# Moving a sum to VectorE, staggering the last weight preparations and re-weighting the list schedule of a four-layer graph kernel

## The chip, the cores and the metric

One core of a Trainium2 chip runs the whole program. The metric is the device time of that core in microseconds (us), from the first to the last instruction of one execution. Engines are named as in the profile: PE is TensorE (PEld its weight loads), DVE is VectorE, ACT is ScalarE, POOL is GpSimd, SP is SyncE, which issues all DMA transfers here.

## The reference

Four graph layers are applied one after the other to 128 graphs of 64 nodes with 512 features, each followed by a residual and a normalisation over the features. All is fp32.

```python
x = _layernorm(x + _L0_gnn_ref(x, adj, w, a))                    # A @ x @ w, A from tanh/exp of x@w@a
x = _layernorm(x + _L1_gnn_ref(x, adj, Wq, bq, Wk, bk, Wv, bv))  # adj*exp(q k^T), normalised, @ v
x = _layernorm(x + _L2_gnn_ref(x, adj, nodemask, Wqk, Wv))       # a softmax weight per node, times x @ Wv
x = _layernorm(x + _L3_gnn_ref(x, adj, W1, b1, gamma, beta, W2, b2))
# _L3: relu(hypergraph_conv(x, adj, W1, b1)) (512 -> 1024), layer_norm,
#      hypergraph_conv(h, adj, W2, b2) (1024 -> 512), + x
```

## The kernel before

Two tiles of 128 rows (four graphs) make a group; there are 32 groups, and the adjacency is prepared for two groups at a time (a "chunk"). Each large product (left side times weights) is made in Strassen's way: the left side and the weights are cut into 2 x 2 blocks, four sums are formed of the left blocks and four of the weight blocks, and seven products replace eight. Sums of the weights are made once, stored in DRAM, and then streamed through a ring of buffers for every group. Products with `v2` (layer 2), `3a` and `3b` (layer 3) take stored weights; those of `m1` and `m2` stay on the chip.

The program is a list of operations with a cost and a key, which a list scheduler written in the kernel orders when it is built. It decides, per engine, the fixed order of the instructions, and which buffer each value gets. The costs only set that order: on the chip each engine takes its instructions in the order found, and waits in front of each until its inputs and its buffer are there.

```python
class Order:
    LATENCY = {"PE": 260, "DVE": 110, "ACT": 130, "POOL": 160, "SP": 2200}   # ns until others see a result
    BYTES_PER_NS = 230
    AHEAD = 3.5
    ...
def w_dve(n):  return 165 + n * 33 // 32      # ns of an operation on n elements per partition
def w_act(n):  return 175 + n * 27 // 32
def w_pool(n): return 200 + n * 9 // 4
    ...
    kind("x", 6, GT, D)
    kind("k4", 13, PIECE)       # 13 buffers of 128 x 1024 fp32: raw weights, transposed x, sums, z, v
    kind("ring", 8, PIECE)      # streamed weights
    ...
def side_sums(a, s, n):                       # the four sums of the left side
    def do(engine, out, left, right, add=False):
        def emit():
            e = nc.vector if engine is dve else nc.gpsimd
            (e.tensor_add if add else e.tensor_sub)(out[1](), left[1](), right[1]())
        engine(n, [left[0], right[0]], [out[0]], emit)
    do(dve, s[0], a["21"], a["22"], True)
    do(pool, s[2], a["11"], a["21"])
    do(dve, s[1], s[0], a["11"])
    do(dve, s[3], a["12"], s[1])

def stored_in_place(which, b, n, width):      # b: the raw quarters, which lie in k4 buffers
    store = in_dram(which, width)
    for k in USE:
        if k[0] == "b": store(k, b[k])        # a DMA to DRAM
    t = {"t1": b["b11"], "t3": b["b12"], "t2": b["b22"], "t4": b["b21"]}
    combine(b, t, n)                          # the sums, in place: three on DVE, one on POOL
    for k in USE:
        if k[0] == "t": store(k, t[k])
    ...
order.key = 7.0
stored_in_place("v2", quarter_views(raw(wv2, 2), D), D, HALF)   # two k4 buffers
order.key = 8.0
stored_in_place("3a", quarters(w3a), PIECE, PIECE)              # four k4 buffers
order.key = 9.0
w3b_q = quarters(w3b)                                           # four more
...                                     # PE: a row of beta times w3b (7 us); DVE: gamma times w3b, in place
stored_in_place("3b", w3b_q, PIECE, PIECE)
    ...
def normalized(...):                          # bn_stats, bn_aggr on DVE, a power on POOL, then ACT:
    act(n // n_stats + 60, ...)               # x * rstd + nm
```

A group goes through steps 0 to 15 of its own (0 to 2 layer 0, 3 to 6 layer 1, 7 to 11 layer 2, 12 to 15 layer 3), and a new group starts every four steps, so about four groups are under way at once. The steps that the prediction speaks of: 7 transposes the normalised x, 8 multiplies by `m2`, 11 by `v2`, 12 gathers the normalised x over the graph (PE, output `bank<-g_bd,x`), 13 multiplies by `3a`, 14 gathers the normalised h (`bank<-g_bd,h`), 15 multiplies by `3b`.

Of the kernel before, what the change touches and what calls it, by code (L numbers as in the profile page):

```python
# [12 lines left out]
AF = mybir.ActivationFunctionType  # L13
# [3 lines left out]
P = 128  # L17
B, N, D, DH = 128, 64, 512, 1024
# [8 lines left out]
PIECE = 1024  # L27
# [25 lines left out]


class Order:
    LATENCY = {"PE": 260, "DVE": 110, "ACT": 130, "POOL": 160, "SP": 2200}
    BYTES_PER_NS = 230
    AHEAD = 3.5

# [107 lines left out]


def w_dve(n):
    return 165 + n * 33 // 32  # L170


def w_act(n):
# [8 lines left out]
def kernel(  # L182
# [23 lines left out]
    nc = tc.nc  # L206
# [10 lines left out]
    def kind(name, n, *shape, space=None):  # L217
        kinds[name] = [(space or sbuf).tile([P, *shape], FP, name=f"{name}{i}") for i in range(n)]

    kind("x", 6, GT, D)  # L220
    kind("k4", 13, PIECE)
    kind("ring", 8, PIECE)
    kind("h", 1, GT, DH)
    kind("k2", 3, D)
# [11 lines left out]
    order = Order({k: len(v) for k, v in kinds.items()})  # L236

    def const(t_, cells=1):
        b = Buf(None, cells)
        b.t = t_  # L240
        return b
# [5 lines left out]
    def dve(n, reads, writes, emit, urgent=0.0):  # L247
        order.add("DVE", w_dve(n), reads, writes, emit, urgent)

    def act(n, reads, writes, emit, urgent=0.0):  # L250
        order.add("ACT", w_act(n), reads, writes, emit, urgent)
# [52 lines left out]
    def load_adj(c):  # L304
        order.key = APART * GC * c - 7.0 if c else -10.5
        adjs[c] = Buf("adj")
        load(adjs[c], adjT[:, ts(c, CT * N)], lambda t_: t_.rearrange("p t i -> p (t i)"))


    def raw(w, n, kind_="k4"):  # L310

        made = []
        v = w.rearrange("(h c p) o -> h p c o", h=n, p=P)
        for h in range(n):
            b = Buf(kind_, 2)
            order.add("SP", 60, [], [b], lambda b=b, h=h: nc.sync.dma_start(out=rows_of(b, w.shape[1]), in_=v[h]),
                      size=4 * P * 1024)
            made.append(b)
        return made

    def rows_of(b, cols):
        return b.t.rearrange("p (c o) -> p c o", o=cols)
# [51 lines left out]
    HALF = PIECE // 2  # L374
# [11 lines left out]
    def quarter_views(bufs, cols):  # L386

        return {
            f"b{h + 1}{i + 1}": (
                bufs[h][i],  # L390
                lambda h=h, i=i: rows_of(bufs[h], cols)[:, :, ts(i, cols // 2)],
            )
            for h in range(2) for i in range(2)
        }
# [3 lines left out]
    def in_dram(which, width):  # L398
        n = PIECE // width
        tiles = []  # L400
        for i in range(-(-len(USE) // n)):
            tiles.append(const(dram.tile([P, PIECE], FP, name=f"{which}_{i}"), n))
        stored[which] = [(t_, min(n, len(USE) - n * i)) for i, t_ in enumerate(tiles)]

        def store(k, piece):
            i = USE.index(k)
            dst = tiles[i // n]

            def emit():
                src = piece[1]()  # L410
                d_ = dst.t[:, ts(i % n, width)].rearrange("p (c o) -> p c o", c=src.shape[1])
                nc.sync.dma_start(out=d_, in_=src)

            order.add("SP", 60, piece[0] if isinstance(piece[0], list) else [piece[0]], [dst[i % n]], emit,
                      size=P * width * 4)

        return store

    def stored_in_place(which, b, n, width):

        store = in_dram(which, width)
        for k in USE:
            if k[0] == "b":
                store(k, b[k])
        t = {"t1": b["b11"], "t3": b["b12"], "t2": b["b22"], "t4": b["b21"]}
        combine(b, t, n)
        for k in USE:
            if k[0] == "t":
                store(k, t[k])
# [64 lines left out]
    m2 = gram("m2", wq2_raw, wk2_raw)  # L494

    order.key = 7.0
    stored_in_place("v2", quarter_views(raw(wv2, 2), D), D, HALF)

    def quarters(w):

        rows, cols = w.shape
        v = w.rearrange("(h c p) (i o) -> h i p c o", h=2, p=P, i=2)
        made = {}
        for h in range(2):
            for i in range(2):
                q = Buf("k4")
                order.add("SP", 60, [], [q],
                          lambda q=q, h=h, i=i: nc.sync.dma_start(out=rows_of(q, cols // 2), in_=v[h, i]),
                          size=P * PIECE * 4)
                made[f"b{h + 1}{i + 1}"] = (q, lambda q=q: rows_of(q, cols // 2))  # L510
        return made
# [7 lines left out]
    bw_b = const(sb("bw_b", D))  # L519
# [149 lines left out]
    def side_sums(a, s, n):  # L669


        def do(engine, out, left, right, add=False):
            def emit():
                e = nc.vector if engine is dve else nc.gpsimd
                (e.tensor_add if add else e.tensor_sub)(out[1](), left[1](), right[1]())

            engine(n, [left[0], right[0]], [out[0]], emit)

        do(dve, s[0], a["21"], a["22"], True)
        do(pool, s[2], a["11"], a["21"])  # L680
        do(dve, s[1], s[0], a["11"])
        do(dve, s[3], a["12"], s[1])

    def left_side(xT):
        a = left_blocks(xT)
# [74 lines left out]
    def normalized(reads_of, view, n_stats, eps, n):  # L760

        mv = Buf("col", GT)
        for t in range(GT):
            st = Buf("col", n_stats)
            for i in range(n_stats):
                dve(n // n_stats, [reads_of(t, i)], [st[i]], lambda t=t, i=i, st=st: nc.vector.bn_stats(
                    st.t[:, 6 * i : 6 * i + 6], view()[:, t, ts(i, n // n_stats)]))
            dve(12, [st], [mv[t]], lambda t=t, st=st: nc.vector.bn_aggr(mv.t[:, 2 * t : 2 * t + 2], st.t[:, : 6 * n_stats]))
        ve, rstd, nm = Buf("col"), Buf("col"), Buf("col")

        def pairs_of(b, i):
            return b.t[:, : 2 * GT].rearrange("p (t s) -> p t s", s=2)[:, :, i]

        dve(GT, [mv], [ve], lambda: nc.vector.tensor_scalar(ve.t[:, :GT], pairs_of(mv, 1), eps, None, ALU.add))
        order.add("POOL", 790, [ve], [rstd],
                  lambda: nc.gpsimd.tensor_tensor(rstd.t[:, :GT], ve.t[:, :GT], mhalf, ALU.pow))
        dve(GT, [mv, rstd], [nm], lambda: nc.vector.scalar_tensor_tensor(
            nm.t[:, :GT], pairs_of(mv, 0), -1.0, rstd.t[:, :GT], ALU.mult, ALU.mult))
        for t in range(GT):
            for i in range(n_stats):  # L780
                act(n // n_stats + 60, [reads_of(t, i), nm, rstd], [reads_of(t, i)], lambda t=t, i=i: nc.scalar.activation(
                    view()[:, t, ts(i, n // n_stats)], view()[:, t, ts(i, n // n_stats)], AF.Identity,
                    bias=nm.t[:, t : t + 1], scale=rstd.t[:, t : t + 1]))

# [25 lines left out]
    def z_into(zT, bias=None):  # L810


        def at(k):
            return xT_view(zT)[:, ts(int(k[1]) - 1, KC // 2), ts(int(k[0]) - 1, P)]

        def cell(k):
            return zT[GT * (int(k[1]) - 1) + int(k[0]) - 1]

        def two(ps):
            return ps().rearrange("p (c q) -> p c q", c=2)  # L820

        def first(k, token, ps):
            if bias is None:
                act(2 * P, [token], [cell(k)], lambda: nc.scalar.copy(at(k), two(ps)), NOW)
            else:
                for c in range(2):
                    col = 2 * (int(k[1]) - 1) + c
                    act(P, [token, bias], [cell(k)], lambda c=c, col=col: nc.scalar.activation(
                        at(k)[:, c], two(ps)[:, c], AF.Identity, bias=bias.t[:, col : col + 1]), NOW)

        def more(k, token, ps):
            dve(2 * P, [token, cell(k)], [cell(k)], lambda: nc.vector.tensor_add(at(k), two(ps), at(k)), NOW)

        return first, more


    def run(g):
        V, A = nc.vector, nc.scalar
# [121 lines left out]
        dve(GT, [mx], [mx], lambda: V.tensor_scalar(mx.t[:, :GT], mx.t[:, :GT], -SCALE, None, ALU.mult), NOW)  # L960
        e2 = Buf("e", GT)
        for t in range(GT):
            act(P, [ps_p, mx], [e2[t]], lambda t=t: A.activation(
                e2.t[:, t, :], tiles(ps_p)[:, t, :], AF.Exp, bias=mx.t[:, t : t + 1], scale=SCALE), NOW)
        dve(GT * N, [e2], [sw], lambda: V.tensor_reduce(sw.t[:, :GT], e2.t, AX.X, ALU.add))
        dve(GT, [sw], [sw], lambda: V.reciprocal(sw.t[:, :GT], sw.t[:, :GT]))
# [14 lines left out]
        for t in range(GT):  # L981
            c = Buf("k2")
            cells = xt[[2 * t, 2 * t + 1]]
            col = own.start + t
            act(D, [bw_b, g1, gT3], [c], lambda c=c, col=col: A.activation(c.t, bw_b.t, AF.Identity, scale=g1.t[:, col : col + 1]))
            pool(D, [c, b3b_b], [c], lambda c=c: nc.gpsimd.tensor_add(c.t, c.t, b3b_b.t))
            pool(D, [c, cells], [cells], lambda c=c, t=t: nc.gpsimd.tensor_add(xt.t[:, t, :], xt.t[:, t, :], c.t))

# [114 lines left out]
```

## Time and profile before

| | |
|---|---|
| time, 3 runs | 2479.0 us median (2472.4 to 2480.49) |
| profiled span | 2468.7 us, granted PE clock 0.986 |
| busy: PEld, ACT, POOL | 1888.6 us (77%), 876.5 us (36%), 619.5 us (25%) |
| DMA | 471.37 MB, mean 191 GB/s |
| sums of left sides on POOL | 128x256: 128 of 933 ns; 128x512: 32 of 1424 ns |
| ACT normalising x, 128x512 | 256 of 808 ns |

The busy shares are of the whole span. An instruction is named by what it writes and reads (`k<-chx` reads the accumulator `chx` and writes a `k` buffer; all `k...` kinds have lost their numbers). In a timeline each row has the start, the busy time, the engine, the operation, its operands and shapes, and in square brackets the idle time of the engine before it with what ended it. The view of waits sums these idle times by who was waited for.

### The profile page before, as it was taken

What the parts mean: (1) busy time and instruction counts of PE and PEld (TensorE: products, weight loads), DVE (VectorE), ACT (ScalarE), POOL (GpSimd) and SP (SyncE); (2) the same over time, 40 slices, a digit from 0 to 9 for tenths busy, and PEclk for the clock granted to TensorE, in tenths of its full rate; (3) what the DMA queues carried; (4) which work ended last, traced back from release to release, by engine and by line L of the source; (5) the groups of instructions that cost most, each with busy time, mean ns of one, the idle gap of its engine ahead of it and who ended that gap; (6) DMA issues with size and microseconds to landing.
All of it is one profiled execution on the core that took longest, in us unless ns stands there. A gap on an engine that the chain in (4) does not pass through costs nothing.

```text
span 2468.7 us, 40059 instructions
## 1 busy us (share of the span) xinstructions
PE 2351.2 (95%) x14984; PEld 1888.6 (77%) x14984; DVE 1674.6 (68%) x3860; ACT 876.5 (36%) x1779; POOL 619.5 (25%) x627
## 2 busy tenths in 40 slices
PE   7888999999999999999999999999999999999997
PEld 4766778877778887777887777888777788777775
DVE  6665667676766777676677767767767676756554
ACT  1322333433343333333333343333334334334332
POOL 3221222221322322232232223223122222212221
PEclk9989999999999999999999999999999999999998
DMA  8645566565557566556656555655655665654554
GB/s 273 233 154 166 176 205 195 185 209 198 172 181 225 170 193 211 188 166 209 203 172 217 191 184 172 223 183 185 218 176 175 204 197 183 201 184 155 191 179 136
DMA packets 156239, 471.37 MB, mean 191 GB/s; under 512 B 17808, under 2 KB 27280, under 8 KB 156048
## 3 DMA queue, kind: packets, MB, share of 16 engines
q1 hardware_dynamic: 156048, 468.82, 57.8%
q8 instruction: 120, 1.97, 0.3%
q14 instruction: 71, 0.58, 0.1%
HBM read 439.13 MB, written 29.62 MB: 190 GB/s over the span
## 4 chain that ended last, share of the span: by engine, by line
PE 77%; DVE 10%; DMA 3%; ACT 2%; POOL 2%; issue 1%; SPq 0%; ACTq 0%; POOLq 0%
PE bank L1040 32%; PE chx L1040 27%; PE chz L1040 18%; DVE col L1040 3%; DVE k L1040 3%; DMA adj<-in_adjT_dram 2%; DVE x L1040 1%; DVE k L604 1%; ACT x L1040 1%; POOL x L1040 1%; POOL k L1040 1%; ACT k L1040 1%; DVE col L960 0%; DVE h L1040 0%; DVE k L605 0%
## 5 line engine op out<-in xcount | busy, mean ns | idle before, releaser
L1040 PE MATMUL chx<-ring,k 128*128 128x256 f32 (+1 forms) x1664 | 478.0, 416 | 0.0
L1040 POOL TENSOR_TENSOR col<-col,mhalf 128x2 f32<-128x2 f32 x160 | 120.6, 754 | 1332.9 <-DVE col L1040 1304.1
L1040 PE MATMUL bank<-ring,k 128*128 128x256 f32 (+1 forms) x1536 | 439.4, 416 | 0.0
L1040 ACT ACTIVATE x<-x,col,col 128x512 f32<-128x512 f32 x256 | 197.7, 808 | 647.4 <-DVE col L1040 647.4
L1040 PEld LDWEIGHTS chx<-ring,k 128*128 128x128 f32 x1664 | 310.3, 191 | 84.7 <-issue 49.6
L1040 PEld LDWEIGHTS bank<-ring,k 128*128 128x128 f32 x1536 | 290.7, 191 | 83.2 <-issue 48.2
L1040 ACT COPY k<-bank 128x512 f32<-128x512 f32 (+1 forms) x416 | 228.3, 573 | 126.1 <-PE bank L1040 122.9
L1040 PE MATMUL chz<-ring,h 128*128 128x256 f32 (+1 forms) x768 | 241.3, 450 | 0.0
L1040 DVE SCALAR_TENSOR_TENSOR x<-chx,col,x 128x256 f32<-128x256 f32 x384 | 175.9, 480 | 93.8 <-PE chx L1040 88.4
L1040 PE MATMUL chx<-k,m 128*128 128x128 f32 x1536 | 207.3, 279 | 10.9 <-ACT k L1040 10.9
L1040 PEld LDWEIGHTS chz<-ring,h 128*128 128x128 f32 x768 | 145.8, 190 | 74.4 <-issue 60.7
L1040 PE MATMUL chz<-ring,k 128*128 128x256 f32 x768 | 199.9, 383 | 0.1
L1040 PEld LDWEIGHTS chx<-k,m 128*128 128x128 f32 x1536 | 188.5, 194 | 14.6 <-ACT k L1040 12.3
L1040 PE MATMUL chx<-ring,h 128*128 128x256 f32 (+1 forms) x640 | 181.2, 422 | 0.0
L1040 DVE BATCH_NORM_STATS2 col<-x 128x6 f32<-128x512 f32 x256 | 175.1, 684 | 3.2
L1040 PEld LDWEIGHTS chz<-ring,k 128*128 128x128 f32 x768 | 144.1, 191 | 28.7 <-issue 9.7
L1040 POOL TENSOR_TENSOR k<-k 128x256 f32<-128x256 f32 x128 | 119.4, 933 | 147.4 <-ACT k L1040 142.8
L1040 PEld LDWEIGHTS chx<-ring,h 128*128 128x128 f32 x640 | 121.5, 190 | 44.6 <-issue 31.4
L1004 ACT ACTIVATE h<-h 128x512 f32<-128x512 f32 x128 | 80.7, 630 | 208.9 <-DVE h L1040 201.8
L1040 PEld LDWEIGHTS bank<-g_bd,h 128*128 128x128 f32 x1024 | 121.7, 198 | 42.1 <-ACT h L1040 29.3
L1040 PE MATMUL bank<-g_bd,h 128*128 128x128 f32 x1024 | 127.5, 284 | 23.2 <-DVE k L605 14.1
L1040 PE MATMUL bank<-k,m 128*128 128x128 f32 x1024 | 137.1, 277 | 8.5 <-ACT g_bd L1040 4.7
(138 smaller groups left out, 3477.4 us busy)
## 6 DMA issues: line engine op xcount, KB each, us to landing
ring<-3a SPq DMA_DIRECT2D x224, 512.0 KB, 4.3
ring<-3b SPq DMA_DIRECT2D x224, 512.0 KB, 4.3
ring<-v SPq DMA_DIRECT2D x189, 512.0 KB, 4.8
ring<-w SPq DMA_DIRECT2D x93, 512.0 KB, 4.8
x<-in_x_dram SPq DMA_DIRECT2D x32, 512.0 KB, 3.7
out_dram<-x SPq DMA_DIRECT2D x32, 512.0 KB, 7.3
ring<-v SPq DMA_DIRECT2D x63, 256.0 KB, 4.7
ring<-w SPq DMA_DIRECT2D x31, 256.0 KB, 4.2
```

The lines of the kernel that those rows point to most:

```text
L604: dve(7 * W, [dn], [dn], lambda: V.reciprocal(flat(dn.t), flat(dn.t)), NOW)
L1004: act(D + 60, [at_h[k][0]], [at_h[k][0]], lambda k=k: A.activation(at_h[k][1](), at_h[k][1](), AF.Relu))
L1040: made = f(*args, **kwargs)
```

## The change

It does three things. All four sums of a left side go to DVE, and the one that POOL made comes last. The preparations of the last three weights (`v2`, `3a`, `3b`) take turns: a token that each claims with its first load and that each of its stores reads lets the next one's first load be scheduled after the last store of the one before it; there are 15 instead of 13 `k4` buffers. And the costs that the list scheduler reckons with (latencies, DVE's cost, several of ACT's) are set nearer to what the profile shows, which gives another order of instructions. It is meant to take a slow operation off POOL, to let fewer raw weights hold buffers at the same time, and to make the schedule fit the chip.

```diff
-    LATENCY = {"PE": 260, "DVE": 110, "ACT": 130, "POOL": 160, "SP": 2200}
+    LATENCY = {"PE": 220, "DVE": 70, "ACT": 60, "POOL": 60, "SP": 2200}
...
 def w_dve(n):
-    return 165 + n * 33 // 32
+    return 175 + n * 35 // 32
...
-    kind("k4", 13, PIECE)
+    kind("k4", 15, PIECE)
...
+    in_turn = const(None)
...
-    def raw(w, n, kind_="k4"):
+    def raw(w, n, kind_="k4", first=()):
...
-            order.add("SP", 60, [], [b], lambda b=b, h=h: nc.sync.dma_start(out=rows_of(b, w.shape[1]), in_=v[h]),
+            order.add("SP", 60, [], [b, *(first if h == 0 else ())],
+                      lambda b=b, h=h: nc.sync.dma_start(out=rows_of(b, w.shape[1]), in_=v[h]),
                       size=4 * P * 1024)
...
-            order.add("SP", 60, piece[0] if isinstance(piece[0], list) else [piece[0]], [dst[i % n]], emit,
-                      size=P * width * 4)
+            order.add("SP", 60, [piece[0], in_turn], [dst[i % n]], emit, size=P * width * 4)
...
-    stored_in_place("v2", quarter_views(raw(wv2, 2), D), D, HALF)
+    stored_in_place("v2", quarter_views(raw(wv2, 2, first=[in_turn]), D), D, HALF)
...  # in quarters()
-                order.add("SP", 60, [], [q],
+                order.add("SP", 60, [in_turn] if made else [], [q] if made else [q, in_turn],
...  # in side_sums()
-        do(dve, s[0], a["21"], a["22"], True)
-        do(pool, s[2], a["11"], a["21"])
-        do(dve, s[1], s[0], a["11"])
-        do(dve, s[3], a["12"], s[1])
+        do(s[0], a["21"], a["22"], True)
+        do(s[1], s[0], a["11"])
+        do(s[3], a["12"], s[1])
+        do(s[2], a["11"], a["21"])
...  # ACT costs: normalising x or h, z with a bias, exp of layer 2, beta row of layer 3
-                act(n // n_stats + 60, [reads_of(t, i), nm, rstd], ...
+                act(n // n_stats + 240, [reads_of(t, i), nm, rstd], ...
-                    act(P, [token, bias], [cell(k)], ...
+                    act(P + 100, [token, bias], [cell(k)], ...
-            act(P, [ps_p, mx], [e2[t]], ...
+            act(P + 40, [ps_p, mx], [e2[t]], ...
-            act(D, [bw_b, g1, gT3], [c], ...
+            act(D + 130, [bw_b, g1, gT3], [c], ...
```

## The prediction

> **What bounds the kernel now.** I read the page's busy shares and slices first:
>
> ```profile
> span 2468.7 us, 40059 instructions
> ...
> PE 2351.2 (95%) x14984; PEld 1888.6 (77%) x14984; DVE 1674.6 (68%) x3860; ACT 876.5 (36%) x1779; POOL 619.5 (25%) x627
> ...
> PE   7888999999999999999999999999999999999997
> ...
> PEclk9989999999999999999999999999999999999998
> ```
>
> PE is the engine that sets the time, and the low digits stand at both ends. A busy PE is not a PE at its peak, since matmuls overlap, so I took the distances between the starts of successive matmuls from the trace: 216 ns for 128x256, 112 for 128x128, 429 for 128x512 are the medians by shape. Every matmul at its shape's median comes to 2355 us. Add 9.6 us before the first one (the first adjacency load), and the span minus this is about 104 us: all that better ordering could ever win, at unchanged PE work. Binned by start, the excess over the medians is 14 us in the first 100 us, 33 in the second, 4 in the third, some 20 in all from 300 to 2300, and 25 in the last 170. So there are three places: weight preparation near 100 to 200 us, small repeated waits, and the drain.
>
> The waits of PE, whole span, longest first (columns: total us, times, longest):
>
> ```profile
> PE bank L1040 <- ACT x L1040: 29.4, 32, 4.5
> PE bank L1040 <- DVE k L605: 16.4, 14, 2.4
> PE chx L1040 <- ACT k L1040: 10.9, 6, 5.3
> PE bank L1040 <- DMA adj<-in_adjT_dram: 9.6, 1, 9.6
> ...
> PE bank L1040 <- DVE k L599: 7.4, 12, 1.2
> ```
>
> The longest single one after the start-up is followed on three engines (timelines of PE, ACT and SP):
>
> ```profile
> 109.80 1.03 PE L1040 MATMUL bank<-ring,k 128*128 128x256 f32 x4
> 116.12 2.08 PE L1040 MATMUL chx<-k,m 128*128 128x128 f32 x8 [5.30 <-ACT k L1040]
> ```
> ```profile
> 115.44 0.63 ACT L1040 ACTIVATE k<-chx,u_c 128x128 f32<-128x128 f32 x2 [12.16 <-DMA 3a<-k]
> ```
> ```profile
> 110.41 3.61 SPq L1040 DMA_DIRECT2D 3a<-k  x4
> ```
>
> ACT could not empty an accumulator because its target, a `k4` buffer, was still being stored as a piece of `3a`; PE then stood for 5.30 us. The eight matmuls after it take 1.87 us to the next row where the same row takes 0.89 in the steady part: the clock record shows half speed from 115.0 to 121.8 us. Its other half-speed stretches here are 145.7 to 152.6, 162.8 to 176.5 and 190.1 to 196.9.
>
> In the steady part the waits between 400 and 1100 us (ten groups) sum to 16.8 us, of which the gather of step 12 is the most regular, once a group (timelines of PE, POOL and DVE in one group):
>
> ```profile
> 406.27 2.13 PE L1040 MATMUL bank<-g_bd,x 128*128 128x128 f32 x16 [0.69 <-ACT x L1040]
> ```
> ```profile
> 402.96 0.98 POOL L1040 TENSOR_TENSOR k<-k 128x256 f32<-128x256 f32 x1
> ```
> ```profile
> 403.27 0.95 DVE L1040 TENSOR_TENSOR k<-k 128x256 f32<-128x256 f32 x1
> 404.14 0.41 DVE L1040 TENSOR_TENSOR k<-bank,k 128x256 f32<-128x256 f32 x1
> ```
>
> The last three rows show the sums: the DVE sum that meets POOL's takes 0.95 us, the PSUM one after it, of the same size, 0.41.
>
> **What the Trainium skill says.** "SBUF — State Buffer", section "SBUF: two separate sides", describes the port pair of VectorE and GpSimd as an exclusive lock: a DVE operation with two SBUF inputs and a GpSimd operation that reads SBUF do not share it, the later one stands. The rows above agree (0.95 against 0.41). "TensorE: Matmul & The Clock Gate", Part 1, says that the array falls to half clock after an idle window and needs about 3.4 us of sustained work to come back; the record here has only 1.0 and 0.5, in multiples of 3.41 us, so each long wait costs about half of a low stretch more. "Perfetto Trace Analysis", "Identifying the Most-Contended Engine", warns that matmul occupancy does not measure headroom; here 95% busy hides 33 us lost between 100 and 200 us.
>
> **The change part by part.**
>
> *Sums on DVE.* Today's DVE sums cost, per group of 32: 192 of 539 ns and 96 of 632 ns (128x256 into `k`), 32 each of 426, 826 and 1376 ns (128x256 into `h`), 32 each of 910, 680 and 679 ns (128x512): 320.6 us, 10.0 per group. After it they are 16 of 128x256 and 4 of 128x512. Undisturbed ones take 0.41 and 0.68 (the lowest in the trace), so 16 x 0.41 + 4 x 0.68 = 9.3 us. DVE gets a quarter more sums and should not get busier: the lock's waiting paid for them. POOL loses 128 x 933 + 32 x 1424 ns = 165 us and goes to about 455. DVE's two-column operations, 285 and 295 ns in the mean with 170 and 150 undisturbed, get a little shorter too. Neither engine sets the end, and PE waits on no POOL sum in the list of waits, so I count 0 for PE.
>
> *One weight at a time, 15 buffers.* The order of SP's queue shows it: the first loads of `3a` and of `3b` stood at places 55 and 61, before the last stores of `v2` and all of `3a`; now they stand at 61 and 80, each behind the stores of the one before. At most four raw quarters hold `k4` buffers instead of up to eight, of 15 and not 13. The wait of 5.30 us should go, with half of the 6.83 us at low clock: -8.7. The stretch after it (142 to 195 us) has PE waits of 3.28 behind a `3b` sum on DVE (one of 2.37 us, met by POOL's of 2.46), 2.37, 0.98, 4.46, 0.68, 0.94 and 2.88: 15.6 us; half clock costs about 10 more after them. Work and POOL's part remain, only spread, so I take half: -12.7. Against it stands that `3b` comes later. In PE's order its beta row was 73 us of matmul work (216 ns per 128x256 and so on) ahead of the first `3b` product, now 39 us; seven products then come one by one among others until 66 us. The chain is 4 scalings of 0.35 us, a store (3.8 us to land), a load (4.3) with SP's waits, under 20 us for the first, so 39 is enough, but SP's queue is in order and can be held by one store: +5.
>
> *New weights of the schedule.* ACT normalises x in 808 ns; the schedule believed 657 (175 + 572 x 27/32) and now 809. In the order, 6.2 us of PE work stood between a group's last product of step 11 and its gather of step 12, each group alike; now 6.2 and 7.1 alternate. The wait there is 0.66 us on average (6.6 us in ten groups), less than the 0.9 added: gone in about 13 groups, -8.6. The other recurring waits, those for the reads of banks at L605 and L599 in the chunk's preparation, keep their place in the order (four bank products in a row and then the next), so 0. In the drain the PE order is the same but for one gather of step 14 moved behind a product, and the waits of 3.8, 3.9 and 5.3 us there are for a serial chain: 0.
>
> Sum: -8.7 - 12.7 + 5 - 8.6 = -25.0 us. 2479.0 - 25.0 = 2454.0 us.
>
> **The rivals.**
>
> *DVE becomes the wall at the transposes.* It takes over the fourth sums where it also empties accumulators, and DVE is in order: one sum ahead of an emptying delays the next product by 0.41 us. For it: DVE is at 68%, and at 141 us it held up PE. Against it: the fourth sum comes last, the seventh product alone needs it, and the lock's 0.5 us per meeting goes away. If one such delay a group reached PE, +0.41 x 32 = +13 us: 2467.
>
> *The last weights come too late.* If the staggered chain is held by a store in SP's queue, PE waits once per `3b` piece: seven pieces of a few us, each followed by a low clock. The saving of 21 us near the start turns into nothing or into a loss of 10 to 20: 2470 to 2490. Speaks for it: today's SP issues of two `3b` stores took 11.84 us, held by DVE. Against: PE has other groups' products between the pieces.
>
> *All of it hidden.* If the removed wait was only the first of several (the accumulator freed, then DVE's sums late, then the chunk's preparation), PE stops 5 us later at another place, and only the small waits go: -8 us, 2471.
>
> *More than I count.* If all of the excess between 100 and 200 us went, and the steady waits by half, -33 - 20: 2426.
>
> **Range and chances.** The floor of 2355 + 9.6 plus a drain that stays is near 2400, so 2% (under 2429.4) would need the start-up to be nearly perfect: 0.07. A loss of 2% (over 2528.6) would need 50 us of new waits in an order that keeps the steady pattern: 0.03. The range is 2434 to 2478: the low end is a gain of 45 us, between my sum and the last rival; the high end covers the third rival and most of the second.
>
> **What would show it right or wrong.** POOL near 455 us busy and DVE not above 1690. No wait of ACT for a store of `3a`, and PE's excess from 100 to 200 us under 20 instead of 33. Waits of PE for ACT's x near 20 us instead of 29.4. PE's matmul count and its work unchanged. Wrong would be: a new PE wait of over 3 us for `ring` weights `3b` between 150 and 230 us; steady groups longer than now (70.71 us between the same DVE rows of two groups, at 401.26 and 471.97); DVE waits becoming PE's main releaser.

## The result and the profile after

The changed kernel takes 2413.35 us (median of 4 runs, 2409.97 to 2414.3), against 2479.44 for the kernel before beside it: ratio 0.9737, 95% interval 0.9716 to 0.9757. It is 2.6% faster. I had said 2454, in a range of 2434 to 2478, so the gain is over twice what I counted, and the time lies below the low end.

The page of the changed kernel, its span, busy shares and the slices of PE and of its clock:

```profile
span 2412.5 us, 40195 instructions
...
PE 2338.4 (97%) x14984; PEld 1889.5 (78%) x14984; DVE 1729.0 (72%) x4020; ACT 871.0 (36%) x1779; POOL 457.3 (19%) x467
...
PE   7989999999999999999999999999999999999996
...
PEclk9999999999999999999999999999999999999998
```

The work of PE is the same 14984 matmuls. DVE has 160 instructions more, POOL 160 fewer. DVE is busier by 54 us; I had expected it near its old figure.

The waits of PE in the changed kernel (total us, times, longest us); the source has shifted, so the row of L607 is the one that was L605:

```profile
PE bank L1039 <- DVE k L607: 15.3, 14, 2.2
PE bank L1039 <- DMA adj<-in_adjT_dram: 10.3, 1, 10.3
PE bank L1039 <- ACT h L1039: 9.0, 2, 5.3
PE bank L1039 <- ACT x L1039: 8.3, 3, 5.0
```

ACT's x went from 32 waits to 3, and two rows are gone from the head of the list: ACT's k for `chx` (10.9 us before, 0.2 now) and L599 (7.4 us before, 0.2 now). L605 has kept its place.

Where the time went, marked by the first of the eight matmuls with a single output column (`bank<-ones,e`) that each group has:

| us | before | after | difference |
|---|---|---|---|
| start to group 5 | 440.3 | 423.3 | -17.0 |
| group 5 to group 27 (22 groups) | 1604.3 | 1577.1 | -27.2 |
| group 27 to the end | 424.1 | 412.2 | -11.9 |
| per two groups, groups 8 to 27 (median) | 145.90 | 143.32 | -2.58 |

All three stretches gain. My sum had 16.4 us for the first, 8.6 for the second and nothing for the third. These four measures are used for every kernel below.

The window from 100 to 200 us shows the first stretch. Columns: window, its length, then busy us (and instructions) of PE, PEld, DVE, ACT and POOL, the PE clock, the DMA share and GB/s. First before, then after:

```profile
100.00:200.00 100.00, 79.06 (x507) 68.32 (x506) 57.59 (x131) 24.71 (x60) 26.09 (x23) 0.83 0.40 146
```
```profile
100.00:200.00 100.00, 93.01 (x659) 76.27 (x657) 70.27 (x159) 30.51 (x71) 19.38 (x16) 0.98 0.55 194
```

PE does 659 matmuls where it did 507, and the granted clock rises from 0.83 to 0.98: between 95 and 215 us, the four half-speed stretches of 6.8 to 13.7 us named in the prediction have become three of 3.4, 3.4 and 6.8 us, at 97.6, 128.3 and 206.8 us.

### The profile page after: what moved, and what is told of

It is laid out like the page before. It is cut to its first block, busy times and chain, and to the rows that moved or that the text cites. A ratio compares the mean times of both kernels' runs of the same rounds, so it can differ in the third digit from the quotient of the medians.

```text
span 2412.5 us, 40195 instructions
## 1 busy us (share of the span) xinstructions
PE 2338.4 (97%) x14984; PEld 1889.5 (78%) x14984; DVE 1729.0 (72%) x4020; ACT 871.0 (36%) x1779; POOL 457.3 (19%) x467
## 4 chain that ended last, share of the span: by engine, by line
PE 89%; DVE 7%; ACT 2%; POOL 1%; issue 1%; DMA 0%; SPq 0%; POOLq 0%; ACTq 0%; DVEq 0%
PE bank L1039 40%; PE chx L1039 29%; PE chz L1039 20%; DVE k L1039 2%; DVE col L1039 1%; DVE k L606 1%; ACT x L1039 1%; DVE x L1039 1%; ACT k L1039 1%; POOL k L1039 0%; DVE h L1039 0%; POOL x L1039 0%; DMA mask_c<-in_mask_dram 0%; DVE k L605 0%; DVE k L607 0%
## 5 line engine op out<-in xcount | busy, mean ns | idle before, releaser
L1039 POOL TENSOR_TENSOR col<-col,mhalf 128x2 f32<-128x2 f32 x160 | 115.4, 721 | 1520.2 <-DVE col L1039 1387.7
L1039 PE MATMUL chx<-k,m 128*128 128x128 f32 x1536 | 200.2, 276 | 1.9 <-ACT x L1039 1.1
L1039 PEld LDWEIGHTS bank<-g_bd,h 128*128 128x128 f32 x1024 | 129.5, 200 | 29.1 <-ACT h L1039 23.0
L1039 PE MATMUL bank<-g_bd,h 128*128 128x128 f32 x1024 | 134.1, 286 | 11.3 <-ACT h L1039 9.0
L1039 DVE TENSOR_TENSOR k<-k 128x256 f32<-128x256 f32 (+1 forms) x226 | 137.1, 613 | 5.9 <-ACT k L1039 5.1
L1039 DVE SCALAR_TENSOR_TENSOR x<-chz,col,x 128x256 f32<-128x256 f32 x192 | 92.3, 481 | 67.6 <-PE chz L1039 66.1
```

The lines of the kernel that those rows point to most:

```text
L1039: made = f(*args, **kwargs)
```

## Experiments

Two theories stood at the start. **Lock**: the gain in the steady part comes from taking the fourth sum off POOL, so that DVE's operations no longer meet it. **Order**: it comes from the new costs, which let the list scheduler place one operation of the normalisation differently on DVE. The kernels below are the kernel before or after with hunks of the change put in or left out; "the hunk" means the lines of the diff printed above.

### The three parts alone

`only_sums` has the hunk of `side_sums()` alone, `only_turns` the token and the 15 buffers, `only_costs` the latencies, DVE's cost and ACT's four costs.

```diff
 # only_sums
-        do(pool, s[2], a["11"], a["21"])
+        do(s[2], a["11"], a["21"])          # on DVE, last of the four
 # only_turns
-    kind("k4", 13, PIECE)
+    kind("k4", 15, PIECE)                   # and in_turn in raw(), quarters(), stored_in_place()
 # only_costs
-    return 165 + n * 33 // 32
+    return 175 + n * 35 // 32               # and LATENCY, and ACT's + 180, + 100, + 40, + 130
```

> The kernel before with all four left sums on VectorE (the old GpSimd sum last), nothing else. Lock theory (GpSimd's sum blocks VectorE's small operations of the normalisation through the shared ports, and so PE): the time between the same rows two groups on falls from 145.8 us by over 1.5 us, PE's waits for ACT x fall from 29.4 to under 12 us, about 2450 us in all. Order theory (the new costs of the list schedule took the waits away): at most 0.5 us per two groups, 2470 to 2480 us. Both: the start-up (first 230 us) keeps its 5 us wait, since the buffers are as before.

> The kernel before with the turn token and 15 k4 buffers, nothing else. Both theories: the gain of the start-up alone, 15 to 25 us earlier at the sixth group, the steady part at 145.8 us per two groups as before; 2455 to 2464 us. If the start-up gain needs the new costs as well: 2470 to 2480 us.

> The kernel before with the new costs of the list schedule alone. Lock theory: the sums on GpSimd stay in the way, the time per two groups falls by under 1 us from 145.8: 2462 to 2480 us. Order theory: it falls by 2 us or more, 2440 to 2450 us.

| | time | ratio to before (95%) | to group 5 | per two groups | group 27 to end |
|---|---|---|---|---|---|
| before | | | 440.3 | 145.90 | 424.1 |
| only_sums | 2475.22 | 1.0005 (0.9996 to 1.0014) | 439.4 | 146.4 | 417.7 |
| only_turns | 2448.49 | 0.9908 (0.9893 to 0.9923) | 416.2 | 145.8 | 424.4 |
| only_costs | 2429.2 | 0.983 (0.9815 to 0.9844) | 437.7 | 142.65 | 419.2 |

The turns carry the start (-24.1 us to group 5), and nothing else; whether the token or the two more buffers do it, no run separates. The costs carry the steady part and 5 us of the end. The sums bring nothing in all: 0.5 us more per two groups, 6.4 us less at the end. The lock theory, as it was put, falls here, by one row of waits in `only_sums`, where PE's waits for x were 29.4 us before:

```profile
PE bank L1037 <- ACT x L1037: 46.6, 32, 5.0
```

Taking the sum off POOL made the wait ahead of the gather longer. Why is shown below, with the chain ahead of the gather.

### Two parts at a time

> The changed kernel with the old sums (one of four on GpSimd, and reckoned as such): turns and costs alone. Additive theory (turns 23 us, costs 42 us, sums nothing): 2403 to 2409 us, 142.7 us per two groups. If the sums on VectorE are needed for the gain of the whole: 2415 to 2425 us.

> The changed kernel with the old costs of the list schedule: sums and turns alone. Additive theory: 2446 to 2452 us, 146.3 us per two groups, PE's waits for ACT x above 40 us as with the sums alone. If the sums give something once the start-up is mended: below 2440 us.

> The changed kernel without the turn token and with 13 k4 buffers: sums and costs alone. Additive theory: 2428 to 2436 us, 143.3 us per two groups, the sixth group 20 us later than in the changed kernel.

`no_sums` (turns and costs) took 2409.55 us, ratio 0.9744 (0.9727 to 0.9761), 142.65 us per two groups; `no_costs` 2455.9, 0.9934 (0.9914 to 0.9955), 146.5; `no_turns` 2431.26, 0.9828 (0.981 to 0.9846), 143.3. Each pair is near the sum of its parts: turns and costs alone are -0.92% and -1.7%, together -2.56%. Leaving out the sums costs nothing that these intervals show.

### After's order, the fourth sum back on POOL

The scheduler still believes that the sum is DVE's, so the order on PE and SP is that of the changed kernel: all 14984 matmuls of the two traces come in the same order. ACT's order differs in three places, all after 2100 us.

```diff
-        do(s[2], a["11"], a["21"])
+        do(s[2], a["11"], a["21"], on="gpsimd")   # scheduled as DVE's, emitted on POOL
```

> The changed kernel with the list schedule as it is (the fourth sum still reckoned as VectorE's), but that sum given to GpSimd when it is written out: PE's and SP's orders are the changed kernel's. Lock theory: most of the steady gain goes, 145 us per two groups or more, waits of PE for ACT x come back, 2430 to 2450 us. Order theory: 2413 to 2420 us, 143.3 per two groups.

It took 2423.23 us, ratio 0.9807 (0.9791 to 0.9824). In the steady part it is no slower than the changed kernel (143.1 against 143.3 us per two groups), with POOL's sums back beside DVE's operations. So it is the order that gives the steady gain, and not which engine makes this sum. The loss lies at the end: 14.4 us more from group 27 on (426.6 against 412.2), of which 6.6 had been gained before. From 2000 to 2300 us, PE and then ACT wait in this kernel:

```profile
PE chx L1042 <- ACT k L1042: 8.8, 3, 3.5
ACT k L987 <- POOL x L1042: 15.8, 6, 3.6
```

In the same window the changed kernel has no such wait of PE, and ACT's is

```profile
ACT k L984 <- POOL x L1039: 7.4, 6, 1.6
```

ACT's wait is for its beta row of layer 3, which writes one of three buffers; in the program a buffer is free again only when POOL has added an earlier row from it to x. POOL's order now has the sums in it as well, so POOL comes later, and ACT's z biases (`k<-chx,u_c`), which PE needs, stand behind the beta row. Three times PE stands for that, and each time its clock falls to half for 3.4 us (at 2112.5, 2187.6 and 2262.7 us; the changed kernel has no half-speed stretch there): 8.8 and about 5 us, together near the 14.4. The pattern, a beta row that idles over 1 us with z biases right behind it, stands three times at the end of the kernel before and of `only_turns`, `only_costs` and `no_sums`, and not once in `only_sums`, `no_costs`, `no_turns` and the changed kernel, which have all sums on DVE. So the sums do one thing for the time: they shorten the end.

### What the new costs move

In the steady part (600 to 2000 us) the kernel before has 19 waits of PE for x, 12.6 us in all; `only_costs` has none. The matmul work that PE has between step 11 and the gather of step 12 is the same 6.24 us in `only_costs` as before, so the gain isn't more cover on PE, as I had thought. The chain before the gather is: statistics and aggregate (DVE), a shift (DVE), a power (POOL), the product -mean x rstd (DVE, `col<-col,col`), the normalisation (ACT), the gather (PE). One such chain in the kernel before, from its timelines:

```profile
1056.33 0.81 POOL L1040 TENSOR_TENSOR col<-col,mhalf 128x2 f32<-128x2 f32 x1
1057.42 0.95 DVE L1040 TENSOR_TENSOR k<-k 128x256 f32<-128x256 f32 x1
1058.62 0.89 DVE L1040 SCALAR_TENSOR_TENSOR col<-col,col 128x2 f32<-128x2 f32 x1
1059.55 0.81 ACT L1040 ACTIVATE x<-x,col,col 128x512 f32<-128x512 f32 x1 [1.09 <-DVE col L1040]
1060.41 1.35 PE L1040 MATMUL bank<-g_bd,x 128*128 128x128 f32 x9 [0.64 <-ACT x L1040]
```

The power ends at 1057.14. DVE's order still has a sum (0.95 us, beside POOL's) and a read of an accumulator ahead of the product; it starts 1.48 us after the power's end and takes 0.89 us. The same chain in `only_costs`:

```profile
1041.34 0.81 POOL L1040 TENSOR_TENSOR col<-col,mhalf 128x2 f32<-128x2 f32 x1
1042.75 0.35 DVE L1040 SCALAR_TENSOR_TENSOR col<-col,col 128x2 f32<-128x2 f32 x1
1043.03 0.41 DVE L1040 TENSOR_TENSOR k<-k 128x256 f32<-128x256 f32 x1
1043.30 0.82 ACT L1040 ACTIVATE x<-x,col,col 128x512 f32<-128x512 f32 x1
1044.56 1.61 PE L1040 MATMUL bank<-g_bd,x 128*128 128x128 f32 x13
```

Now the sum stands behind the product, which starts 0.60 us after the power's end and takes 0.35 us, and the gather waits for nothing. From the power's end to the product's end it is 2.37 us in the kernel before and 0.96 in `only_costs` (means of 19 and 20 groups from 600 to 2000 us).

The lock has a part in this after all. Of the 1.41 us between the two, 0.54 is the product itself: in the kernel before it ends within 0.02 us of POOL's x + bias, in `only_costs` within 0.02 us of POOL's sum, which ends sooner. And of the sum's 0.95 us, 0.54 is its meeting with POOL's sum. In `only_sums` POOL's sum is gone, but POOL's x + bias moves up into its place, and the DVE sum in front (by its place in the program, the moved fourth one) meets that for longer: 1.50 us. First the POOL operation with which the product ends in the kernel before, then three rows of `only_sums`:

```profile
1058.05 1.45 POOL L1040 TENSOR_TENSOR x<-x,bv_b 128x512 f32<-128x512 f32 x1
```
```profile
1057.45 1.52 POOL L1037 TENSOR_TENSOR x<-x,bv_b 128x512 f32<-128x512 f32 x1
1057.76 1.50 DVE L1037 TENSOR_TENSOR k<-k 128x256 f32<-128x256 f32 x1
1059.51 0.89 DVE L1037 SCALAR_TENSOR_TENSOR col<-col,col 128x2 f32<-128x2 f32 x1
```

So the order decides which operations of DVE meet one of POOL's, and it is the meeting that makes them long. No kernel here runs this chain with nothing on POOL beside it. In the changed kernel only every second group has the new order: in the others a sum (1.37 us) still stands ahead of the product, and these are the groups with 7.1 us of matmul work ahead of the gather.

The wait at L599 went by a second pair on DVE. In the kernel before, from 400 us on, 11 of 12 reads at L599 stand behind L591, which prepares the adjacency of the next chunk and waits for its load (0.33 to 1.37 us), while the bank to be read is ready (DVE, then PE):

```profile
949.37 0.29 DVE L591 TENSOR_SCALAR kept<-adj 128x256 f32<-128x256 f32 x1 [0.83 <-DMA adj<-in_adjT_dram]
949.58 0.41 DVE L599 TENSOR_TENSOR k<-bank,eye 128x256 f32<-128x256 f32 x1
```
```profile
950.05 0.70 PE L1040 MATMUL bank<-k,same 128*128 128x256 f32 x2 [0.66 <-DVE k L599]
```

In `only_costs` and in the changed kernel the read comes ahead of it in every chunk. The list of waits names DVE; what PE waited for was a DMA.

The distances between the starts of matmuls, summed per two groups, give what both were worth: the products ahead of the gather (`chz<-k,m`) 8.81 to 7.16 us, the chunk's product ahead of the one that waits for L599 (`bank<-kept,same`) 1.23 to 0.43, the gather itself 3.94 to 3.57; with smaller ones, some of them longer, the whole -3.25.

### Which of the costs

```diff
 # cost_of_vector_ops: the kernel before with this alone
-    return 165 + n * 33 // 32
+    return 175 + n * 35 // 32
 # cost_of_scalar_ops: + 180 (normalising), + 100 (z), + 40 (exp), + 130 (beta row) alone
 # latencies_only: LATENCY alone
```

> Before with one line changed: the schedule's cost of a VectorE operation of n elements, from 165 + 33n/32 to 175 + 35n/32. Theory (order): this one line is what puts the normalisation of step 11 ahead of the next group's sum on VectorE, so it alone gives the steady gain: 142 to 143.5 us per two groups, ScalarE's wait for x ahead of the gather of step 12 gone from the steady part, time 2430 to 2442 us. Rival (it needs ScalarE's higher costs or the shorter latencies as well): 145.5 to 146.5 us per two groups and 2460 to 2480 us.

> Before with ScalarE's four kinds of costs as in the change (normalisation +180 ns, z +100, exponential +40, beta row +130), VectorE's and the latencies as before. Theory (order by VectorE's costs): the sum still stands ahead of the normalisation on VectorE, 145 to 146.5 us per two groups, 2460 to 2480 us. Rival (ScalarE's costs carry the gain): 142 to 143.5 us per two groups and 2430 to 2442 us.

> Before with the five latencies of the schedule shortened as in the change and nothing else. Theory (order by VectorE's costs): nothing in the steady part, 145 to 146.5 us per two groups, 2460 to 2482 us. Rival (the latencies carry the gain): 142 to 143.5 us per two groups and 2430 to 2442 us.

| | time | ratio to before (95%) | per two groups |
|---|---|---|---|
| cost_of_vector_ops | 2447.13 | 0.989 (0.9875 to 0.9905) | 144.24 |
| cost_of_scalar_ops | 2462.98 | 0.9958 (0.9941 to 0.9974) | 145.44 |
| latencies_only | 2456.46 | 0.9934 (0.9912 to 0.9957) | 145.64 |

The theory missed on the first: half of the steady gain, not all. DVE's cost alone does move both pairs on DVE. ACT's x and L599 are gone from PE's steady waits there, as they should be, but a new one has come, once in two groups (13.4 us from 600 to 2000). Its timelines:

```profile
1127.14 1.33 POOL L1040 TENSOR_TENSOR x<-x,k 128x512 f32<-128x512 f32 x1
1128.51 0.72 ACT L985 ACTIVATE k<-bw_b,col 128x512 f32<-128x512 f32 x1 [3.22 <-POOL x L1040]
1129.14 0.61 ACT L1040 ACTIVATE k<-chx,u_c 128x128 f32<-128x128 f32 x2
1129.80 1.16 PE L1040 MATMUL chx<-k,m 128*128 128x128 f32 x8 [1.34 <-ACT k L1040]
```

ACT stands for 3.22 us on the beta row of one group (`k<-bw_b,col`), held until POOL's sum into x, and behind it in ACT's order lie the z biases of another group (`k<-chx,u_c`), whose accumulator PE needs. In `only_costs` the z biases come first in every group of the steady part. So one more pair of operations was in the wrong order, on another engine. Two more kernels ask which cost sets it right.

> Before with VectorE's and ScalarE's new costs and the old latencies. Theory (two orders: VectorE's cost puts the normalisation ahead of the next group's sum, ScalarE's costs put the z biases ahead of the beta row, which stood waiting for GpSimd's x in cost_of_vector_ops): both waits gone, 142.4 to 143.2 us per two groups, 2426 to 2440 us. Rival (the shortened latencies are needed for the second): 144 to 145.5 us per two groups, 2442 to 2452 us.

> Before with VectorE's new cost and the shorter latencies, ScalarE's costs as before. Theory (two orders): PE still waits some 1.3 us for ScalarE's z in every second group, 144 to 144.6 us per two groups, 2436 to 2448 us. Rival (the latencies take that wait away): 142.4 to 143.2 us per two groups, 2424 to 2434 us.

`vector_and_scalar_costs` took 2423.59 us, ratio 0.9785 (0.9768 to 0.9802), 142.44 us per two groups; `vector_costs_and_latencies` 2450.59, 0.9897 (0.9881 to 0.9913), 144.41, with 11.7 us of the wait for the z biases left. In the first, two rows are all that PE waits for from 600 to 2000 us:

```profile
PE bank L1040 <- DVE k L605: 9.6, 10, 1.0
PE bank L1040 <- DVE col L919: 2.5, 9, 0.3
```

DVE's cost and ACT's costs are needed together: alone they give 1.1% and 0.4%, together 2.15%. The latencies give something alone (0.66%; where, its profile does not tell: it is of the longest of six executions, which reached from 2449.1 to 2466.16 us, and has group 5 9.4 us earlier and the end 7.1 us longer) and take something away beside the other two: `only_costs`, which has them, is 0.983, without them it is 0.9785. Which of ACT's four costs turns the pair on ACT I did not try.

### The wait that the change left

L605 (L607 after) is PE waiting for DVE to read the banks of the chunk's preparation: between the reads lies a reciprocal of 1.75 us, in order. Three edits tried to take it away, from `no_sums` or from the changed kernel.

```diff
 # no_sums_bank_free: the first bank is read once, and no more after the reciprocal
-   reciprocal(dn, dn);  dn = (ps_d > 0) * dn
+   reciprocal(hw, dn);  dn = (dn > TINY) * hw
 # no_sums_scalar_copy: in addition, the second bank
-   t2 = ps_h * dn                      # DVE
+   t2 = copy(ps_h)                     # ACT
+   t2 = t2 * dn                        # DVE, from SBUF
 # no_sums_reciprocal_last, all_reciprocal_last: the copy on DVE, ahead of the reciprocal
+   t2 = copy(ps_h)                     # DVE
    reciprocal(hw, dn);  dn = (dn > TINY) * hw;  t2 = t2 * dn
```

> Turns and costs alone, and in the preparation of a chunk the reciprocal no longer in place, so that the test for a positive sum reads the SBUF copy and the PSUM bank comes free before the reciprocal of 1.75 us. If PE's remaining regular wait (for DVE at the line of that test, 1.0 us per two groups, 15 us in all) is for that bank: 10 to 15 us faster than without it. If it is DVE's order that PE waits for, whatever bank: within 3 us of it.

> The kernel no_sums_bank_free with one thing more: ScalarE copies the second PSUM bank of the chunk step to SBUF, and VectorE multiplies from there, so that no bank waits behind the reciprocal. Theory (the wait of some 10 us at the chunk step in the steady part is the reciprocal standing ahead of the reads of a bank): the wait is gone and 9 to 13 us of the time with it, 2392 to 2397 us. Rival (PE then waits for the next thing that VectorE does after the reciprocal): within 3 us of no_sums_bank_free, 2402 to 2408 us.

> The kernel no_sums, with VectorE copying the second PSUM bank of the chunk step to SBUF ahead of the 1.75 us reciprocal and not behind it, and nothing given to another engine. Theory (the wait of some 10 us at the chunk step is the reciprocal ahead of the reads of a bank, and the scalar copy lost its gain only by the places that the list gave to other ScalarE work): 5 to 13 us faster than no_sums, 2396 to 2404 us. Rival (whatever stands behind the reciprocal waits as long, or the list moves elsewhere): 2405 to 2430 us.

> The same edit made in the changed kernel, with its sums on VectorE. Theory: 5 to 13 us faster than the changed kernel, 2400 to 2408 us. Rival: 2410 us or more.

`no_sums_bank_free` took 2405.37, ratio 0.9731 (0.9712 to 0.975): the steady part is unchanged at 142.65, since the wait (9.7 us now, 9.6 before) went over to the next bank, L610. The other three lost: 2435.84 (0.984, 0.9826 to 0.9855), 2441.43 (0.9863, 0.9844 to 0.9882) and 2432.51 (0.9823, 0.9807 to 0.984). The waits of `no_sums_reciprocal_last` from 600 to 2000 us:

```profile
PE bank L1043 <- ACT k L1043: 16.3, 20, 2.1
PE bank L1043 <- DVE k L1043: 5.2, 5, 1.0
PE bank L1043 <- DVE k L605: 1.6, 5, 0.3
PE bank L1043 <- DVE k L608: 1.5, 5, 0.3
```

The banks' own wait did fall, from 9.6 to 3.1 us, but one new operation in the list gave another order, which repeats only every four groups: the time per two groups, taken at each group in turn, runs 156.3, 142.6, 133.7, 147.5, together 290.0 per four groups against 285.3. The copy on ACT does much the same (13.7 us of waits for ACT's k), though it burdens another engine. So the reciprocal does hold the banks; which placement of the new order makes ACT late was not found.

### Without sums and latencies, and the whole change again

```diff
 # turns_and_two_costs: the change less two hunks
     LATENCY = {"PE": 260, "DVE": 110, "ACT": 130, "POOL": 160, "SP": 2200}   # as before
         do(pool, s[2], a["11"], a["21"])                                     # as before
```

> The turns of the last weights with VectorE's and ScalarE's new costs, the old latencies and the fourth sum left on GpSimd. Theory (the parts add up; the sums bring nothing and the latencies some us less than nothing): vector_and_scalar_costs less the 20 us that the turns took off only_costs, 2400 to 2407 us, 142.4 to 142.8 us per two groups, and some 8 us faster than the whole change on the same chip. Rival (the sums on VectorE carry part of the whole change's gain): no faster than the whole change, 2412 us or more.

> The whole change, unaltered, beside turns_and_two_costs on the same chip. Theory: 2410 to 2415 us as before, 0.973 to 0.975 of the kernel before, and slower than turns_and_two_costs by 5 to 12 us. Rival: within 3 us of it.

Measured on one chip: 2402.97 us, ratio 0.9702 (0.9684 to 0.972), for the first; 2412.8, 0.9741 (0.9723 to 0.9759), for the whole change. The intervals do not meet; it beats both kernels. Its page:

```profile
span 2401.9 us, 40212 instructions
...
PE 2325.8 (97%) x14984; PEld 1881.6 (78%) x14984; DVE 1668.7 (69%) x3860; ACT 867.9 (36%) x1779; POOL 608.1 (25%) x627
```

Against the whole change its profile is 3.5 us shorter to group 5, 0.88 us per two groups shorter after that (142.44 against 143.32), and 3.1 us longer at the end. `no_sums`, which differs from `turns_and_two_costs` by the latencies alone, parts the two: of the 0.88, 0.67 is the sums' and 0.21 the latencies'. By these profiles, of different chips, the sums save 7.0 us at the end (419.1 against 412.1) and cost 10.7 before it; the latencies cost 5.8 us, most of it at the end.

## Why the prediction was wrong

**The new weights of the schedule: the step that failed.** I put them at -8.6 us; alone they measured 1.7%, 42 us. Two things in the step were wrong. The mechanism was "6.2 and 7.1 alternate", more PE work ahead of half of the gathers. `only_costs` has 6.24 us there as before, and yet no wait at all in the steady part: the place of one 0.15 to 0.9 us operation on DVE decided it, in every group and not in "about 13 groups". In the changed kernel the 7.1 us do stand ahead of half of the gathers, but there they cover a sum that still lies in front; the other half lost its wait with 6.2. I had compared the order on PE, not that on DVE and ACT, where the chain runs. And "L605 and L599 ... keep their place in the order ..., so 0" was right for L605 (16.4 to 15.3) and wrong for L599 (7.4 to 0.2, 0.8 us per two groups by the distances), whose place on DVE had changed. The size was also too small because I took the wait for the loss: 0.66 us of idle time in the mean was 0.83 us of distance (1.65 per two groups), since a row of eight matmuls is listed with 1.06 us where the next one starts after 0.89, and an idle time is counted only from the end of the 1.06. The gather behind it got faster as well.

**One weight at a time: right in cause, too small in size.** The wait of 5.30 us for the store of `3a` is gone. ACT's idle time ahead of the z biases, first before and then after, no longer names the store:

```profile
L1040 ACT ACTIVATE k<-chx,u_c 128x128 f32<-128x128 f32 x128 | 40.1, 365 | 62.2 <-PE chx L1040 49.9 <-DMA 3a<-k 12.2
```
```profile
L1039 ACT ACTIVATE k<-chx,u_c 128x128 f32<-128x128 f32 x128 | 40.1, 365 | 70.6 <-PE chx L1039 70.5
```

Measured by `only_turns`, the part is -22.7 us (0.92% of 2471.7), where -8.7 - 12.7 + 5 gave -16.4. The excess over the medians of the shapes between 100 and 200 us fell from 35.8 to 10.9 there (counted with one median for each shape; the prediction had 33), and from 200 to 300 us it did not rise (7.8 to 5.6). So "I take half" was too timid, and the +5 for late `3b` loads did not come; the second rival is refuted. In the whole change the window from 100 to 200 us has 12.8 of excess, under my line of 20.

**Sums on DVE: 0 for PE held, the reason did not.** `only_sums` is 1.0005, a balance of 4.8 us lost from group 5 to 27 and 6.4 won at the end, so that the 0 is in part luck. POOL came to 457.3 us, as worked out. DVE was to stay under 1690 and is at 1729.0. It got not "a quarter more sums" but a third (20 a group for 15). Three of its groups after the change (busy us, mean ns):

```profile
L1039 DVE TENSOR_TENSOR k<-k 128x256 f32<-128x256 f32 x224 | 135.7, 612 | 5.9 <-ACT k L1039 5.1
L1039 DVE TENSOR_TENSOR k<-k,k 128x256 f32<-128x256 f32 x192 | 108.1, 563 | 4.3
L1039 DVE TENSOR_TENSOR h<-k 128x256 f32<-128x256 f32 x32 | 38.7, 1208 | 33.3 <-ACT k L1039 33.3
```

With the other sums these make 413.7 us, 12.9 per group, not 9.3 of "undisturbed" ones: POOL's bias and residual operations on 128x512 are still there to be met. The first rival, DVE as the wall, could show only in the 0.67 us per two groups between `no_sums` and the whole change, 0.34 per group, near the 0.41 it had named. But of these only 0.2 goes when POOL makes the sum in the same order (`after_sum_on_pool`, 143.1); the rest is the order.

**The end: 0 was wrong.** Group 27 to the end is 11.9 us shorter. `only_costs` has -4.9 of it and `only_sums` -6.4; I had argued from the order of PE alone, while beta rows on ACT, which waited for POOL, held up the z biases. What gives the 4.9 was not followed. The two waits for h of the last group (9.0 us) are the serial chain, and they stayed.

**The sum and the range.** Parts alone: -22.7, -42 and +1, in all -64 of 2479, near the measured -66. The rival "More than I count" (2426) had the right direction, but it was 13 us short. "All of it hidden" (2471) did not happen: in the whole change the removed waits were not followed by others. The "floor ... near 2400" rests on a sum that does not come out: the 14984 matmuls of the trace before, each at the median of its shape, make 2261 us and not 2355, and the excess from 300 to 2300 us is 101 us and not "some 20". The change took 27.2 us between groups 5 and 27 alone, more than the 20 I had left there to be won. The chance of 0.07 rested on this count, by which only the start-up had much to give. Of the signs I named for a loss, a new wait for `3b` and longer steady groups did not appear. The third did in part: PE's longest row is now DVE's L607, not because it grew (16.4 to 15.3) but because the others went; in sum ACT's rows (28.5 us) are still more than DVE's (23.4). "PE's waits for x near 20" came out at 8.3.

## What to carry to other kernels

Where a list scheduler fixes the order on in-order engines, compare the old and new order on the engines of the dependence chain (here DVE's statistics and ACT's biases), not only on the engine that sets the time: a short operation behind a sum cost 0.8 us in each group. A cost change of a few per cent, or one extra operation, can turn a steady order into another 1 to 2% away in either direction, so take each group of costs alone and in pairs, and keep the ones that help: here the turns and two of three kinds of costs beat the whole change. Where a wait names an engine, look at what that engine itself stood for: one of the waits for DVE was a DMA's. A removed wait of PE can be worth more than its idle time in the list of waits; the distance between the starts of matmuls gives its price.

## What the runs showed of the hardware that I had not expected

DVE operations of two columns are held up by POOL's large ones as well. In the changed kernel's timelines, first POOL and then DVE:

```profile
1027.85 1.27 POOL L1039 TENSOR_TENSOR x<-x,bv_b 128x512 f32<-128x512 f32 x1 [3.32 <-ACT k L1039]
1030.00 1.52 POOL L1039 TENSOR_TENSOR x<-x,bv_b 128x512 f32<-128x512 f32 x1
```
```profile
1028.30 0.85 DVE L1039 TENSOR_SCALAR col<-col 128x2 f32<-128x2 f32 x1
1030.74 0.80 DVE L1039 SCALAR_TENSOR_TENSOR col<-col,col 128x2 f32<-128x2 f32 x1
```

Both end within 0.03 us of POOL's operation (1029.15 after 1029.12, 1031.54 after 1031.52), while the same forms take 0.17 and 0.15 us undisturbed. That fits the exclusive lock of the Trainium skill's "SBUF — State Buffer", section "SBUF: two separate sides", in which the one that comes second blocks while the other's whole instruction runs. The page names DVE operations in a two-port mode or with two SBUF inputs; the second row has two inputs, and which mode the one-input TENSOR_SCALAR ran in no run shows. In both rows the price of the meeting is POOL's remaining time, however small DVE's operation is. It lies on the chain ahead of the gather, and moving the sums off POOL does not remove it, since POOL's x + bias is the partner.
